# Convolutional mixer on one core: image loads on GpSimd's queue, projection units in eights, and reordered short chains

## The chip, the cores and the metric

The kernel runs on one core of a Trainium2 chip. TensorE (PE in the profile) multiplies matrices into PSUM; VectorE (DVE), ScalarE (ACT) and GpSimd (POOL) work on tiles; SyncE (SP) issues most DMA transfers, ACT and POOL some. The metric is the device time of one execution in microseconds. Three executions of the kernel before gave 3662.24, 3666.53 and 3667.2; the time before is the median, 3666.53 us.

## What is computed

The input is eight images of 384 channels by 32 x 32 positions, in float32. Four layers follow, each `x + f(GroupNorm(x))`:

- layer 0: q, k and v are each a depthwise 3x3 convolution, batch norm over all eight images, exact gelu and a 1x1 convolution; attention over the 1024 positions in 8 heads of 48; an output projection with batch norm over all images;
- layer 1: a gate takes the 2 best of 4 experts for each image; an expert is two 1x1 convolutions with an activation between;
- layer 2: a depthwise 3x3 convolution and a 1x1 convolution, both with weights rounded to -1, 0 and 1;
- layer 3: deformable attention. A depthwise 5x5 convolution of stride 2 on q, gelu and a 1x1 convolution give offsets (through tanh); the image is sampled bilinearly at 16 x 16 shifted points; keys and values come from the samples; 6 heads of 64 attend; a projection follows.

Both batch norms of layer 0 join all images: what follows one cannot start before the last image has gone through what precedes it. An image is 1.57 MB and lies in SBUF as 128 partitions by KC = 3 chunks of 1024.

## The kernel before

**Convolution stage (0 to 366 us).** For each image `norm(b)` gives three functions: `begin` (statistics of the three chunks on DVE by `gn_start`, then `gn_mean`), `middle` (`gn_spread`: matmul `gna`, L115, and two DVE operations) and `end` (`gn_scale`: matmul `gnb`, L126, the power -0.5 on POOL in `rsqrt`, L96, the shift `ss` on DVE, L131; then `affine` on ACT, L145, into one of two padded images `pads`). `stack(b, g)` copies 42 channels, three times shifted by a row, from a pad to a tile `st` of 126 partitions (three DMAs on SP's queue, L319); `left_over` (L340) collects the six channels that nine such groups leave, for four images at a time. A group of `st` is multiplied by a banded weight `cw[:, g]` in 12 matmul instructions of 512 columns (L404), copied by ACT (L410), measured by DVE (L412) and written to `raw` in DRAM, by ACT's DMA queue and for three groups of the last image by POOL's (L427). For every second image, the last three groups are computed on DVE instead (`convolve`, `tap`, L291; `finish`, L298, writes `cst` by SP's queue at L301).

The loop over `work` goes through (image, group) pairs. `stacks(n)` issues copies up to `AHEAD` = 9 groups ahead. `begins` says at which group's turn the next image's `norm` begins; its three functions follow one per turn, and the image after it is then loaded if it is not yet (`load_x`, L241, by `load_image`, L168 to L170). [...] Before this loop stands the order that the change touches:

```
        stacks(2)
        with tc.issue_after(stacked[0].ins):
            load_x(1)
            nc.sync.dma_start(out=cw[:, 3:], in_=i["cw"][:, 3:])
            ident = load_const("ident")
        stacks(AHEAD)
        load_x(2)
```

The first three groups' weights `cw[:, :3]` are loaded at L244, directly behind the first image. `ident` is a 128 x 128 identity used only in a branch not taken.

**Attention (375 to 1785 us).** An image has four pairs of head blocks `pr`, two halves h of the queries and four steps kc of two key blocks each: 32 steps. In a step PE does the scores of the next step (`scores`, L676), ACT the exponential (L683), PE the weighting (`weigh`, L691). Other matmuls of PE lie in a list `todo`: projections of q and k (`project`, L593), values (`values`, L566), the output projection of the image before (`out_project`, L613). At the second step of every half (`kc == NS`, L773), up to four units are taken from it. A unit is three accumulating products, six instructions in the trace, and its result is copied from PSUM by `evac` (ACT or DVE in turn, L77, L79) or DVE. `GELUS` (L561) names the steps of an image, counted from 0, at which ACT applies gelu to a third of the next image (`gelu_chunk`).

**Joint (1785 to 1810 us).** After the last output projection `out_project` with a given `po` copies a bank on ACT, measures it on DVE and sums products with x (`cross`, L509). `norms` (L817 to L850) aggregates with `bn_moments` (L155), makes batch-norm scales and group-norm scales for every image with the matmuls `gmean` and `gvar`.

**Layers 1 to 3 (1810 to 3665 us).** Layers 2 and 3 of image b are a generator; each `yield` gives an estimate of microseconds in which PE is free, and after it as many units of layer 1 of image b + 1 are put in as 2.6 us (`UNIT`) fit. The nine depthwise taps of layer 2 (L1416, L1424) on DVE precede `yield 2.0` (L1426) and the pointwise matmuls `pw` (L1432). In layer 3 the offset products `pom` (L1565) go through tanh on ACT to y, x and mask rows; DVE scales each and adds its grid (L1575, and one `tensor_scalar` after it); ACT forms `1 - |distance|` for x (L1583, L1584) and for eight blocks of y (`wt`, L1597, L1598), POOL multiplies both (L1599), and PE samples with `wt` (`xsb`, L1603). In images 0 to 5 the offset products take one small matmul and go through DRAM. The last two images have no layer 1 beside them and run as a pair. The output's last projection `pf` (L1759) ends in a DVE sum per chunk (L1763) and a DMA per chunk (`put`, L1770).

## Time and profile before

| what | value |
|---|---|
| median of three executions | 3666.53 us |
| profiled execution, its own time | 3666.73 us |
| span of the profile | 3664.9 us |
| mean granted TensorE clock | 0.983 |
| PE busy | 3542.1 us, 97% |
| DVE busy | 1759.0 us, 48% |
| ACT busy | 1268.3 us, 35% |
| POOL busy | 214.0 us, 6% |
| PE busy in 0 to 92, 92 to 184, 184 to 275, 275 to 367 us | 61.42, 83.51, 88.66, 91.40 us |

A line of the timeline gives the start, the time that a run of like instructions took, engine, source line, operation, what it writes and reads, how many, and in brackets the idle time of the engine just before it with what ended it. A matmul product in float32 shows as several instructions. "Waits" add up such idle times by the pair of waiting and releasing work. In a table of windows, busy times of the engines stand first, then the granted TensorE clock as a share, the DMA engines' busy share and the bytes moved per second. The span starts at the first instruction; the execution's own time also holds what lies around it.

### The profile page before, as it was taken

The numbers are of one execution on the slowest core, as the hardware profiler recorded it, in microseconds if no ns is written. First come the engines' busy times: TensorE is split into PE (matmuls) and PEld (weight loads), VectorE is DVE, ScalarE is ACT, GpSimd is POOL, SyncE is SP. The second block draws the span as 40 slices with busy tenths as digits, with TensorE's granted clock in tenths as the row PEclk, the third lists the DMA queues.
The fourth block names the chain that finished last, engine by engine and source line by source line (L and its number), as shares of the span: only waits on it lengthen the run. The fifth ranks groups of instructions, "written<-read, shape, count | busy, mean of one in ns | idle before, by whom it ended". The sixth has DMA issues, their size and how long they took to land.

```text
span 3664.9 us, 38838 instructions
## 1 busy us (share of the span) xinstructions
PE 3542.1 (97%) x15533; PEld 1520.4 (41%) x15533; DVE 1759.0 (48%) x2823; ACT 1268.3 (35%) x1512; POOL 214.0 (6%) x194
## 2 busy tenths in 40 slices
PE   6999999999999999999899999999999999999888
PEld 3444333333333333334444444445344444444434
DVE  6687123242323232323446547474664647557563
ACT  2222454545444454543322321323322232322222
POOL 0101100000000000000000010100102010010112
PEclk9999999999999999999999999999999999999898
DMA  6677211121212021212440010111101001010000
GB/s 227 229 259 274 73 55 52 49 64 38 63 42 78 25 76 27 74 28 74 146 183 23 33 52 21 39 49 34 38 24 56 26 34 49 22 54 19 0 35 18
DMA packets 88746, 252.79 MB, mean 69 GB/s; under 512 B 19754, under 2 KB 20418, under 8 KB 88170
## 3 DMA queue, kind: packets, MB, share of 16 engines
q1 hardware_dynamic: 74832, 210.82, 17.3%
q10 hardware_dynamic: 12120, 37.19, 2.9%
q8 instruction: 127, 2.08, 0.2%
q0 software_dynamic: 1600, 2.15, 0.2%
q14 instruction: 67, 0.55, 0.0%
HBM read 133.44 MB, written 75.59 MB: 57 GB/s over the span
## 4 chain that ended last, share of the span: by engine, by line
PE 40%; DVE 9%; ACT 1%; DMA 0%; issue 0%; POOL 0%; DVEq 0%; POOLq 0%; ACTq 0%; SPq 0%
PE y L1349 12%; PE ph L1328 8%; DVE y L1424 6%; PE pq L1469 3%; PE pf L1759 3%; PE pw L1432 3%; PE pav L1659 2%; PE s L1643 2%; DVE hd L1314 1%; PE pss L1672 1%; PE pk L1617 1%; PE pv L1626 1%; PE xsb L1603 1%; PE px L1492 1%; DVE off L1539 1%; PE plog L1078 0%
## 5 line engine op out<-in xcount | busy, mean ns | idle before, releaser
L683 ACT ACTIVATE p<-s 128x1024 f32<-128x1024 f32 x512 | 497.0, 1021 | 507.8 <-PE s L676 507.0
L1349 PE MATMUL y<-hd,w_sb 128*128 128x512 f32 x1080 | 491.3, 600 | 3.5 <-DVE hd L1314 3.5
L691 PE MATMUL pav<-p,vt 64*64 64x512 f32 x4096 | 488.9, 590 | 0.0
L1328 PE MATMUL ph<-h,w_sb 128*128 128x512 f32 x1104 | 485.0, 594 | 0.2 <-DMA w_sb<-in_w_dram 0.2
L676 PE MATMUL s<-qk,qk 48*64 48x512 f32 x3072 | 371.8, 597 | 3.4 <-ACT p L683 3.4
L404 PE MATMUL pk<-st,cw_sb 126*126 126x512 f32 x720 | 312.7, 595 | 17.7 <-DMA st<-pad 15.4
L1328 PEld LDWEIGHTS ph<-h,w_sb 128*128 128x128 f32 x1104 | 207.5, 190 | 259.1 <-issue 253.9
L1349 PEld LDWEIGHTS y<-hd,w_sb 128*128 128x128 f32 x1080 | 198.8, 191 | 245.5 <-issue 233.9
L691 PEld LDWEIGHTS pav<-p,vt 64*64 64x64 f32 x4096 | 165.1, 133 | 276.6 <-issue 268.4
L652 DVE COPY ta<-pav 128x512 f32<-128x512 f32 (+1 forms) x65 | 44.3, 682 | 411.1 <-PE pav L691 408.1
L1424 DVE SCALAR_TENSOR_TENSOR y<-h,tap,y 128x961 f32<-128x961 f32 (+1 forms) x192 | 234.8, 1249 | 0.6
L1338 ACT ACTIVATE hd<-ph,b_sb 128x512 f32<-128x512 f32 x180 | 122.7, 682 | 315.7 <-PE ph L1328 315.6
L1539 DVE SCALAR_TENSOR_TENSOR off<-q,dw_sb,off 128x225 f32<-128x225 f32 (+3 forms) x432 | 212.5, 553 | 1.6
L404 PEld LDWEIGHTS pk<-st,cw_sb 126*126 126x126 f32 x720 | 136.8, 192 | 183.0 <-issue 176.7
L676 PEld LDWEIGHTS s<-qk,qk 48*64 48x64 f32 x3072 | 112.5, 133 | 227.5 <-issue 184.2
L79 DVE COPY qk<-pq 128x512 f32<-128x512 f32 x48 | 33.2, 692 | 292.2 <-PE pq L593 292.2
L1650 ACT ACTIVATE p<-s 128x1024 f32<-128x1024 f32 x96 | 93.2, 1021 | 191.0 <-PE s L1643 190.9
L410 ACT COPY y<-pk 126x512 f32<-126x512 f32 (+1 forms) x124 | 69.9, 585 | 237.7 <-PE pk L404 119.0
L1314 DVE TENSOR_TENSOR hd<-hd,cb 128x512 f32<-128x512 f32 x180 | 123.3, 690 | 48.2 <-ACT hd L1338 48.0
L1432 PE MATMUL pw<-y,upw 128*128 128x512 f32 x288 | 129.7, 604 | 9.4 <-DVE y L1424 9.4
L1759 PE MATMUL pf<-att,wp_sb 128*128 128x512 f32 x288 | 130.4, 608 | 4.3 <-DVE att L1686 3.8
L1695 POOL TENSOR_TENSOR p<-p,p 128x1024 f32<-128x1024 f32 x48 | 113.0, 2354 | 355.1 <-ACT p L1650 355.1
(295 smaller groups left out, 3838.9 us busy)
## 6 DMA issues: line engine op xcount, KB each, us to landing
g<-raw SPq DMA_DIRECT2D x72, 512.0 KB
st<-pad SPq DMA_DIRECT2D x180, 168.0 KB
raw<-y ACTq DMA_DIRECT2D x171, 168.0 KB
xa<-in_x_dram SPq DMA_DIRECT2D x24, 512.0 KB
xh<-in_x_dram SPq DMA_DIRECT2D x48, 256.0 KB
f<-in_x_dram SPq DMA_DIRECT2D x24, 512.0 KB
f<-o SPq DMA_DIRECT2D x24, 512.0 KB
o<-ot SPq DMA_DIRECT2D x42, 256.0 KB
```

The source lines that it names most:

```text
L404: nc.tensor.matmul(pk[h].rearrange("p (h w) -> p h w", w=W)[: 3 * nch, :, o0 : o0 + c1 - c0], lhsT=lhs, rhs=rhs, start=(k == 0), stop=(k = ...
L676: nc.tensor.matmul(s[64 * k : 64 * k + 64, j * HALF : (j + 1) * HALF], lhsT=kt[r, k0 : k0 + 64], rhs=qt[r, h * HALF : (h + 1) * HALF], sta ...
L683: nc.scalar.activation(p, s, AF.Exp, scale=scale)
L691: nc.tensor.matmul(pav[k][64 * j : 64 * j + 64, :], lhsT=vts[b % 2][r, kc, 2 * hd : 2 * hd + 2, :].rearrange("p a b -> p (a b)"), rhs=p[r, ...
L1314: nc.vector.tensor_tensor(hd, hd, state["cb"], ALU.mult)
L1328: nc.tensor.matmul(ph, lhsT=w1[:, e, c, dc * P : (dc + 1) * P], rhs=state["h1"][c], start=(c == 0), stop=(c == KC - 1),)
L1338: nc.scalar.activation(hd, ph, AF.Relu, bias=b1[:, k : k + 1])
L1349: nc.tensor.matmul(y, lhsT=w2[:, e, dc, m * P : (m + 1) * P], rhs=state[h, k], start=(k == 0), stop=(k == NE * KC - 1),)
L1424: nc.vector.scalar_tensor_tensor(d, f, tap2[:, c, t : t + 1], d, ALU.mult, ALU.add)
L1432: nc.tensor.matmul(pw[h], lhsT=upw2[:, c, m * P : (m + 1) * P], rhs=y[c][:, hs], start=(c == 0), stop=(c == KC - 1),)
L1539: nc.vector.scalar_tensor_tensor(d, f, dw3[:, t : t + 1], d, ALU.mult, ALU.add)
L1759: nc.tensor.matmul(pf[:, hs], lhsT=wp3[:, pr, m * P : (m + 1) * P], rhs=att[:, pr, hs], start=(pr == 0), stop=(pr == NPAIR3 - 1),)
```

## The change

It has six parts.

1. `load_image` takes a queue. Image 1 is loaded by POOL's queue directly behind `cw[:, :3]`; the remaining weights `cw[:, 3:]` and image 2 go on that queue too, held behind the first and the third stack's copies (`behind`). `ident` moves on SP's queue behind the first nine groups.
2. `begins` starts at -3 instead of -1, so that the first norms may begin up to two turns earlier. Image 3 is then loaded at an earlier turn.
3. In attention up to eight units are taken, at the second half (h = 1) only; `GELUS` moves from steps 9, 13, 17 to 5, 13, 21.
4. At the joint, the three aggregates of the output's batch norm come ahead of the last image's `cross` sums; two of these are held behind the first aggregate.
5. `yield 2.0` becomes 3.5. The offsets' rows come in the order x, y, mask; one DVE operation for each of x and y goes, its scale and shift going into ACT's `Abs` (and into the constant `npos`).
6. The last output chunk of the last image is summed and stored in two halves.

```diff
@@ -152,7 +152,7 @@

     def bn_moments(st, j, tiles):

-        nc.vector.bn_aggr(tiles[0][:, j, :], st[:, j, :, :].rearrange("p a b -> p (a b)"))
+        return nc.vector.bn_aggr(tiles[0][:, j, :], st[:, j, :, :].rearrange("p a b -> p (a b)"))

     def bn_params(g, b, tiles):

@@ -165,9 +165,16 @@
         nc.vector.tensor_tensor(sh, b, sh, ALU.subtract)
         return sc, sh

-    def load_image(dst, src):
-        for c in range(KC):
-            nc.sync.dma_start(out=dst[:, c, :], in_=src[:, c, :])
+    def load_image(dst, src, queue=nc.sync):
+        return [queue.dma_start(out=dst[:, c, :], in_=src[:, c, :]) for c in range(KC)]
+
+    def behind(ins, first):
+
+        tc.add_manual_dep(
+            ins.ins, first.ins.name, mybir.DependencyInfo(
+                mybir.DependencyClass.Sync, mybir.DependencyReason.DATA
+            ), reason="transfers in their order",
+        )

     x_img = [i["x"][b].rearrange("(p c) n -> p c n", c=KC) for b in range(B)]
     out_img = [out[b].rearrange("(p c) n -> p c n", c=KC) for b in range(B)]
@@ -234,14 +241,15 @@
         nc.gpsimd.memset(cst, 1.0)
         xts = {}

-        def load_x(b):
+        def load_x(b, queue=nc.sync):
             xts[b] = image(f"xa{b}")
-            load_image(xts[b], x_img[b])
+            return load_image(xts[b], x_img[b], queue)

         load_x(0)
         g4 = load_const("g4")
         cw = wa.tile([3 * GC, NGC, 3, 3 * GC], F32, name="cw_sb")
         nc.sync.dma_start(out=cw[:, :3], in_=i["cw"][:, :3])
+        load_x(1, nc.gpsimd)
         cwv = load_a("cwv")
         cwr = load_a("cwr")
         vst = wa.tile([3 * GC, 3, 2, 6], F32, name="vst")
@@ -351,7 +359,7 @@
         ]
         work = [(b, g) for b in range(B) for g in groups[b]]

-        begins, n = {}, -1
+        begins, n = {}, -3
         for b in range(1, B):
             n = max(n + 3, work.index((b, groups[b][0])) - AHEAD - 2)
             begins[n] = b
@@ -366,13 +374,15 @@
         for f in norm(0):
             f()

-        stacks(2)
-        with tc.issue_after(stacked[0].ins):
-            load_x(1)
-            nc.sync.dma_start(out=cw[:, 3:], in_=i["cw"][:, 3:])
-            ident = load_const("ident")
+        stacks(1)
+        first = stacked[0]
+        stacks(3)
+        rest = nc.gpsimd.dma_start(out=cw[:, 3:], in_=i["cw"][:, 3:])
+        behind(rest, first)
+        for load in load_x(2, nc.gpsimd):
+            behind(load, stacked[0])
         stacks(AHEAD)
-        load_x(2)
+        ident = load_const("ident")
         gb0 = load_a("gb0")
         sel0, sel1, msk, is_v, one3 = (
             load_a(n) for n in ("sel0", "sel1", "msk", "is_v", "one3")
@@ -477,6 +487,7 @@


     ost = const.tile([P, KC, 2 * B, 6], F32, name="ost")
+    sc_o = bn_tiles(P, KC, "out")
     omv = const.tile([P, B, KC, 2], F32, name="omv")
     xo = const.tile([P, B, KC, 2], F32, name="xo")
     gbo, gw, gbias, ewt, sel2 = (load_const(n) for n in ("gbo", "gw", "gbias", "ewt", "sel2"))
@@ -558,7 +569,7 @@

-        GELUS = {s: [(v, c) for c in range(KC)] for v, s in enumerate((9, 13, 17))}
+        GELUS = {s: [(v, c) for c in range(KC)] for v, s in enumerate((5, 13, 21))}

         def values(b, t):
             pv = bank(f"pv{b}_{t}")
@@ -624,6 +635,8 @@
                 nc.scalar.copy(ot, po)
             nc.vector.bn_stats(ost[:, m, 2 * b + h, :], ot if po_new else po)
             (nc.sync if b + 1 < B else nc.scalar).dma_start(out=o_dram[b, :, m, hs], in_=ot)
+            if not po_new:
+                return lambda: cross(b, m, h, xh, ot)
             cross(b, m, h, xh, ot)

         def spare(k, h):
@@ -769,8 +782,8 @@
                     nc.vector.transpose(spare(1, k), spare(0, k))

             early = b == 0 and pr == 0 and h == 0
-            if early or kc == NS:
-                for _ in range(min(2 if early else 4, len(todo))):
+            if early or (h == 1 and kc == NS):
+                for _ in range(min(2 if early else 8, len(todo))):
                     todo.pop(0)()
             if kc == NT8 - NS:
                 turned = normalise(b, pr, h, pav)
@@ -787,8 +800,14 @@
                         pos[m][:, qs], lhsT=wo0[:, c, m * P : (m + 1) * P],
                         rhs=atts[B - 1][:, c, HALF:][:, qs], start=(c == 0), stop=(c == KC - 1),
                     )
+        ends = [out_project(B - 1, m, 1, pos[m]) for m in range(KC)]
         for m in range(KC):
-            out_project(B - 1, m, 1, pos[m])
+            first = bn_moments(ost, m, sc_o)
+        ends[0]()
+
+        with tc.issue_after(first.ins):
+            for end in ends[1:]:
+                end()

         okt = pp.tile([P, B * NU * 16], F32, tag="p", name="okt")
         recf = rec.rearrange("p u q -> p (u q)")
@@ -803,7 +822,6 @@

-    sc_o = bn_tiles(P, KC, "out")
     _, sco, sho = sc_o
     rs1 = const.tile([P, B], F32, name="rs1")
     sf1 = const.tile([P, B], F32, name="sf1")
@@ -814,8 +832,8 @@
     sum_g = const.tile([P, B], F32, name="sum_g")
     mean_g = const.tile([P, B], F32, name="mean_g")

-    def norms():
-        for c in range(KC):
+    def norms(moments):
+        for c in range(KC if moments else 0):
             bn_moments(ost, c, sc_o)
         bn_params(gbo[:, 0, :], gbo[:, 1, :], sc_o)
         sc, sh = (t.unsqueeze(1).to_broadcast([P, B, KC]) for t in (sco, sho))
@@ -850,7 +868,7 @@
                 sb1[:, :, c], rs1, sho[:, c : c + 1], sf1, ALU.mult, ALU.add
             )

-    norms()
+    norms(False)

@@ -982,7 +1000,7 @@
                         hs = slice(h * HALF, (h + 1) * HALF)
                         nc.vector.bn_stats(ost[:, m, 2 * b + h, :], oe[:, m, hs])
                         cross(b, m, h, xe[:, m, hs], oe[:, m, hs])
-            norms()
+            norms(True)
             for (b, t), f in fetched.items():
                 load_image(f, o_dram[b] if t else x_img[b])

@@ -1423,7 +1441,7 @@
                 f = src[:, r0 + dy : r1 + dy, c0 + dx : c1 + dx]
                 nc.vector.scalar_tensor_tensor(d, f, tap2[:, c, t : t + 1], d, ALU.mult, ALU.add)
                 yield 1.25
-        yield 2.0
+        yield 3.5
         for m in range(KC):
             whole, pw = pair(last, f"pw{b}_{m}")
             for h in range(2):
@@ -1560,28 +1578,31 @@
                 nc.sync.dma_start(out=t, in_=om_dram[b, r : r + 1].to_broadcast([P, NG * LS]))
                 om.append(t)
             yield 7.0
-        for r in range(0 if om else 3):
+        for r in () if om else (1, 0, 2):
             po = big(f"pom_{b}_{r}")
             nc.tensor.matmul(po[:, :512], lhsT=pw3[:, r, :], rhs=offf[:, :512], start=True, stop=True)
             nc.tensor.matmul(po[:, 512:768], lhsT=pw3[:, r, :], rhs=offf[:, 512:], start=True, stop=True)
             t = pl.one([P, NG * LS], f"om{r}", f"om{r}_{b}")

             nc.scalar.activation(t, po[:, : NG * LS], AF.Tanh, scale=1.0 if r < 2 else 0.5)
-            om.append(t)
+            om.insert(0 if r == 0 else r, t)
             yield 0.3
-        gy, gx, md = om
-        for r, t in enumerate((gy, gx)):
+        gx, gy, md = om[1], om[0], om[2]
+
+        for r, t in ((1, gx), (0, gy)):
             t3 = t.rearrange("p (g s) -> p g s", g=NG)
             nc.vector.scalar_tensor_tensor(
                 t3, t3, 2.0 / HS, ref3[:, r, :].unsqueeze(1).to_broadcast([P, NG, LS]),
                 ALU.mult, ALU.add,
             )
-            nc.vector.tensor_scalar(t, t, 1.0, 0.5 * (H - 1), ALU.add, ALU.mult)
+
+            if r == 1:
+                nc.scalar.activation(
+                    gx, gx, AF.Abs, bias=npos[:, NT8 : NT8 + 1], scale=0.5 * (H - 1)
+                )
+                nc.scalar.activation(gx, gx, AF.Relu, bias=1.0, scale=-1.0)
         nc.scalar.activation(md, md, AF.Tanh, scale=0.25, bias=quarter)
         nc.vector.tensor_scalar(md, md, 0.5, 0.5, ALU.mult, ALU.add)
-
-        nc.scalar.activation(gx, gx, AF.Abs, bias=npos[:, NT8 : NT8 + 1])
-        nc.scalar.activation(gx, gx, AF.Relu, bias=1.0, scale=-1.0)
         yield 6.0
         xsb = big(f"xsb_{b}")
         xs2 = vbank(f"xs2_{b}")
@@ -1594,7 +1615,9 @@
             i0, i1 = _sample_rows(t)
             sl = slice(i0 * HS, i1 * HS)
             wt = pl.flat([P, NG, (i1 - i0) * HS], f"wt_{b}_{t}")
-            nc.scalar.activation(wt, gy3[:, :, sl], AF.Abs, bias=npos[:, t : t + 1])
+            nc.scalar.activation(
+                wt, gy3[:, :, sl], AF.Abs, bias=npos[:, t : t + 1], scale=0.5 * (H - 1)
+            )
             nc.scalar.activation(wt, wt, AF.Relu, bias=1.0, scale=-1.0)
             nc.gpsimd.tensor_tensor(wt, wt, gx3[:, :, sl], ALU.mult)
             if t == 0:
@@ -1760,14 +1783,18 @@
                         pf[:, hs], lhsT=wp3[:, pr, m * P : (m + 1) * P], rhs=att[:, pr, hs],
                         start=(pr == 0), stop=(pr == NPAIR3 - 1),
                     )
-            nc.vector.scalar_tensor_tensor(
-                xt[:, m, :], pf, pb3[:, m : m + 1], xt[:, m, :], ALU.add, ALU.add
-            )
-            put(m, xt)
+
+            n = 2 if last and m == KC - 1 else 1
+            for k in range(n):
+                ks = slice(k * N // n, (k + 1) * N // n)
+                nc.vector.scalar_tensor_tensor(
+                    xt[:, m, ks], pf[:, ks], pb3[:, m : m + 1], xt[:, m, ks], ALU.add, ALU.add
+                )
+                put(m, xt, ks)
             yield 0.0

     def put_image(b):
-        return lambda m, xt: nc.sync.dma_start(out=out_img[b][:, m, :], in_=xt[:, m, :])
+        return lambda m, xt, ks: nc.sync.dma_start(out=out_img[b][:, m, ks], in_=xt[:, m, ks])

     UNIT = 2.6

@@ -1844,7 +1871,7 @@
                     out=xt, in_=x2_dram[bass.ds(bi, 1)].rearrange("o p c n -> p (o c) n")
                 )

-                def put_any(m, xt):
+                def put_any(m, xt, ks):
                     nc.sync.dma_start(
                         out=out[bass.ds(bi, 1)].rearrange("o (p c) n -> p (o c) n", c=KC)[
                             :, m : m + 1, :
@@ -1965,7 +1992,8 @@
     L["ref3"] = np.broadcast_to(ref, (P, 2, LS))
     part = np.arange(P)
     pos = [-(part // W + t * (P // W)) for t in range(NT8)] + [-(part % W)]
-    L["npos"] = np.stack(pos, axis=1).astype(f)
+
+    L["npos"] = np.stack(pos, axis=1).astype(f) + f(0.5 * (H - 1))
     return {k: np.ascontiguousarray(v) for k, v in L.items()}
```

## The prediction

> **What bounds the kernel now.** The profile's page gives PE 97% of the span of 3664.9 us; the next engine, DVE, has 48%. So the time is PE's matmuls plus what PE waits, and an edit is worth only what it takes from one of the two. I read the table of PE's waits first, then PE's timeline where those waits lie, then the neighbours that set them.
>
> PE's waits (engine, line, releaser: us in total, times, longest):
> ```profile
> PE gna_a L115 <- DVE mv_a L109: 22.8, 2, 13.7
> PE pk L404 <- DMA st<-pad: 15.4, 2, 8.2
> PE pw L1432 <- DVE y L1424: 9.4, 8, 3.0
> ```
> The first two belong to the convolution stage, 0 to 366 us. PE's timeline there (start, us, line, operation, count, idle before):
> ```profile
> 18.18 11.93 PE L404 MATMUL pk<-st,cw_sb 126*126 126x512 f32 x24 [7.24 <-DMA st<-pad]
> 38.26 7.08 PE L404 MATMUL pk<-st,cw_sb 126*126 126x512 f32 x12 [8.16 <-DMA st<-pad]
> ...
> 60.90 5.29 PE L404 MATMUL pk<-st,cw_sb 126*126 126x512 f32 x12
> ...
> 100.23 0.56 PE L115 MATMUL gna_a<-mv_a,g_sb 128*128 128x2 f32 x2 [13.65 <-DVE mv_a L109]
> 100.66 8.31 PE L404 MATMUL pk<-st,cw_sb 126*126 126x512 f32 x12
> ```
> Two holes, 8.16 us and 13.65 us, and after each the next 12 matmuls are slow: 7.08 and 8.31 us. Steady, a group of 12 starts every 5.15 us (66.17 us on, 48 matmuls in 20.42 us). The windows say why (PE, PEld, DVE, ACT, POOL busy, granted clock, DMA share, GB/s):
> ```profile
> 38.30:45.00 6.70, 6.70 (x12) 3.01 (x13) 2.83 (x4) 0.58 (x1) 0.00 (x0) 0.73 0.68 230
> 100.00:110.00 10.00, 9.77 (x19) 4.65 (x20) 8.35 (x14) 1.17 (x2) 0.55 (x1) 0.66 0.34 113
> ```
> The granted clock is 0.73 and 0.66 there. So a hole costs its length and then 1.93 us (7.08 − 5.15) or 3.16 us (8.31 − 5.15): 8.16 + 1.93 + 13.65 + 3.16 = 26.9 us.
>
> **The first hole: loads off SP's queue.** In the SP timeline the third group's copies (`st`, L319) are issued at 33.44, behind image 1's load (20.33), the rest of `cw` (22.17) and `ident` (33.05), which waited 10.4 us for an ACT-queue write. Afterwards image 1, the rest of `cw` and image 2 go out on POOL's queue, `ident` follows the first nine groups, and SP goes from the first stacks to the next. A group is 3 copies of 168 KB, 0.50 MB; at the stage's some 300 GB/s (below) that is 1.7 us, against 5.15 us of PE. Shared in thirds with ACT's writes and POOL's loads it is 5.0 us: just enough while POOL's 2.7 MB (`cw` rest 1.14, image 2 1.57) last, 27 us. The three groups that land ahead of image 2 are the cover; I charge 1 us (0 to 4), and remove 8.16 + 1.93.
>
> **The second hole: the fourth image.** Image 3's load leaves SP at 89.42, behind 18 copies from 64.10 and the `cst` copies of 84.66; its statistics end on DVE just before 100.23. Afterwards its three DMAs stand between the stacks of groups 6 and 7 of image 1, which I place at 60 to 71 us, so it lands by about 77 us (issue to end took 8.6 us before: 89.42 to 98). PE asks at 86.6 − 8.16 − 1.93 + 4.4 = 81 us. The margin of 4 us holds 5 us of DVE statistics (94.71 to 99.7) only partly: 0 to 5 us may stay. I take 1.5 off: 13.65 + 3.16 − 1.5.
>
> **What the new order delays.** DVE's order in the changed program puts the six statistics of image 1 and their aggregate ahead of the last step of image 0's norm, which before stood here:
> ```profile
> 11.80 0.16 DVE L131 SCALAR_TENSOR_TENSOR ss_a<-ga_a,ss_a 128x1 f32<-128x1 f32 x1 [0.67 <-POOL ss_a L96]
> ```
> Behind it wait ACT's affines (11.99), the first copies (13.26) and PE (18.18): the whole stage. So the kernel cannot start before image 1 has landed. POOL can issue it after its memsets, at 7.16, by 8.7 (0.50 us an issue). 1.57 MB at the 312 GB/s that the window from 2 to 9.5 us shows is 5.0 us, with some 1.2 us of earlier loads ahead: the last chunk lands at about 14.6, two statistics and the aggregate take 1.7, so L131 runs at 16.3 and the start is 4.4 us late. Here a rule speaks against the change. The Trainium skill, "DMA: Bandwidth & Descriptors", section "Issuing engine by pattern", gives simple loads to SP, and GpSimd's path costs about 2.0 us plus bytes/436e3 ("Anatomy of one DMA — SWDGE (gpsimd) path"). An estimate from that page is 3.2 us for the last 512 KB chunk after the others' 2.4 us: landing near 13.5, a delay of 3. This trace's only POOL loads are smaller and slower (KB each, then median us to landing):
> ```profile
> raw<-y POOLq DMA_DIRECT2D x9, 168.0 KB, 7.1
> ```
> 7.1 us for 168 KB, with other traffic, would put the last chunk at 15.8 or, if the bytes add, at 18: a delay of 5.5 to 8. The row is the nearer to a chip with its queues full, but these writes go to DRAM; I keep 4.4 from the byte rate and the range 2 to 8. The first matmuls are equally cold before and after.
>
> Stage sum: 8.16 + 1.93 − 1 + 13.65 + 3.16 − 1.5 − 4.4 = **20.0 us gained** (10 to 25).
>
> **Units in eights (L773).** Between attention steps PE takes blocks of projection units. PE's timeline (matmul groups, all of image 1's kind):
> ```profile
> 625.62 1.90 PE L691 MATMUL pav<-p,vt 64*64 64x512 f32 x16
> 627.45 5.42 PE L613 MATMUL po<-att,wo_sb 128*128 128x512 f32 x12
> 632.71 5.31 PE L593 MATMUL pq<-g,wk_sb 128*128 128x512 f32 x12
> ...
> 645.06 1.90 PE L676 MATMUL s<-qk,qk 48*64 48x512 f32 x16
> 646.78 1.90 PE L691 MATMUL pav<-p,vt 64*64 64x512 f32 x16
> ...
> 650.22 1.90 PE L691 MATMUL pav<-p,vt 64*64 64x512 f32 x16
> 652.05 5.42 PE L593 MATMUL pq<-g,wq_sb 128*128 128x512 f32 x12
> ...
> 664.51 1.90 PE L676 MATMUL s<-qk,qk 48*64 48x512 f32 x16
> ```
> A regular interval is 1.72 us (646.78 − 645.06). From 625.62 to 645.06 are five intervals and 24 matmuls: 19.44 − 8.60 = 10.84. From 650.22 to 664.51, five intervals and 12: 14.29 − 8.60 = 5.69. Twice 5.69 less 10.84 leaves **0.54 us that a block costs whatever its size**. Counting the program's order, 58 blocks become 37: 21 × 0.54 = **11.3 us gained**. The skill's "TensorEngine Tiling (Array Packing)", section "Key Properties", has a reason: changing the tiling mode drains TensorE. Its price is not there; from "TensorE: Matmul & The Clock Gate", section "Single matmul latency", a matmul that cannot overlap costs 166 ns more, and two changes a block make 0.33: 21 × 0.33 = 7.0. The row is measured in place and holds the whole break in the stream, so 11.3. Range 6 to 13.
>
> The cover: the gelu of the next image moves to steps 5, 13 and 21, ahead of such blocks. ACT then does a table load and three gelus, 1.28 + 3.50 us (627.03 to 631.8), before it copies a first unit out of PSUM. PE reaches the bank needing that copy about 5.2 us after the block begins: it fits by 0.4 us. Were it not to fit, 7 images × 2 blocks × up to 1 us; I charge 0. At step 5 the values' gelu also needs its image loaded, 17 us of steps and a block after the load starts: enough for 1.57 MB.
>
> **Statistics before the joint (L624).** The three aggregates of the output's batch norm move ahead of the `cross` sums; the same DVE work stands in another order in one unbroken run (1783.51 to 1790.94), and the chain to `gmean` (7.0 us of PE wait) still needs all of it. 0, ±0.5.
>
> **`yield 2.0` to 3.5 (L1426).** A further result unit of layer 1 (6 matmuls, 2.58 us) comes before the pointwise matmuls, which now wait 1.03 us in six images. That gains some 0.7 each, 4.2. But units run out one earlier: attention's last pair in those images loses its filler, as in the last image, where it waits 0.27 and 0.48 us: −0.75 × 6 = −4.5. Net 0, ±4.
>
> **Offsets (L1575 and on).** Two DVE operations (0.56 + 0.55 us) go, their scale folded into ACT's Abs; the x row comes first. In the last image they stand in the chain to `xsb` (4.40 us wait at 3586.93), of which y's one is hidden by x's ACT steps now started earlier: −0.5. In the image before, DVE's taps bound it: −0.2. Elsewhere layer 1 covers them. Total **0.7** (0 to 2).
>
> **Last chunk in halves (L1763).** The last sum takes 1.28 us (3656.99) and its store is issued at 3658.3, 6.6 us before the span's end. In halves the last sum is 0.69 us (the 128x512 DVE rows) and the last store 256 KB instead of 512 KB: 0.6 + 0.4 = **1.0** (0.3 to 2).
>
> **Sum.** 20.0 + 11.3 + 0 + 0 + 0.7 + 1.0 = 33.0. Span 3664.9 − 33 = 3632; the profiled execution took 3666.73, 1.8 more. The median shown is 3666.53, 0.2 below that execution, so **3634** (3633.5 rounded). Likeliest case's own range: 3626 to 3641.
>
> **Rivals.** (1) The first norm waits 8 us and the fourth image comes 6 us late with a cold clock behind it: the stage gives 26.9 − 8 − 6 − 3 = 10 instead of 20, time 3644. For it: the POOL row above, and SP's semaphore waits on ACT-queue writes (10.4 us at 22.6), which can hit image 3's load again. Against: the DMA share in the two windows, 0.68 and 0.34, leaves room.
> (2) Merging does nothing: PE's break is ACT's evacuation and the exponentials' restart rather than the change of mode, and a longer block meets them as before: 3634 + 11.3 = 3645. For it: ACT's table load of 1.28 us after each gelu block stands in the restart (639.15). Against: the 0.54 also comes out of blocks with copies on DVE (24 matmuls, 128x384: 16.88 us from 669.66).
> (3) It ends slower: POOL's image 1 lands late. Every us of its lateness is a us of PE, since L131 stands behind it in DVE's order. Slower by 7.3 needs 33 + 7.3 = 40 us beyond the assumed 14.6, a landing at 55; at 60 us the time is 3679. For it: POOL's power operation takes 0.55 us at 51.00 but 1.39 at 66.67 while DVE is busy, so POOL is held up at times. Against: the longest POOL landing in the trace is 8.2 us.
> (4) The change doesn't do what it says: both (1) and (2), with image 2's early load taking the bandwidth of the first stacks: 3657 to 3666.
>
> **How the numbers follow.** Likeliest 0.55, (1) 0.20, (2) 0.13, (3) 0.03, (4) 0.09. The range goes from all gains at their bounds (25 + 13 + 4 + 2 + 2 = 46, cut to 44 as they do not all come: 3622) to past (1) and (2): 3650. This kernel's measurement tells 0.2%, 7.3 us. Faster takes in all but (3) and about half of (4): 0.92; same 0.05, slower 0.03.
>
> **What would show it.** Right: PE's row for `st` in the waits under 2 us after the start; the wait for `mv_a` under 6; first L404 at 21 to 26; 37 blocks, block cost 0.5 each; last store of 256 KB. Wrong: a first L404 beyond 28, a new hole at image 3's `gna_a`, PE waiting for a PSUM bank in the first unit of a block, or restarts after eights longer than after fours.

## The result and the profile after

The changed kernel takes 3644.70 us (median of five executions, 3643.82 to 3650.53) against 3666.53 before (five executions, 3662.24 to 3668.54): a ratio of 0.9947, 95% interval 0.9935 to 0.9958. That is 21.8 us faster, where 32.5 were forecast (3634); it lies inside the range of 3622 to 3650, but outside the 3626 to 3641 of the case held likeliest. The profiled span (one execution of each kernel) fell from 3664.9 to 3641.9 us, by 23.0. Marks on PE's timelines cut these 23.0 us into stages:

| stage, from mark to mark | before | after | change | forecast |
|---|---|---|---|---|
| start to first attention scores | 389.75 | 385.10 | -4.65 | -20.0 |
| to the matmul `gmean` (attention and joint) | 1402.80 | 1388.46 | -14.34 | -11.3 |
| to the last image's `pf` (layers 1 to 3) | 1848.68 | 1845.30 | -3.38 | -0.7 |
| to the end of the span (last output) | 23.67 | 23.04 | -0.63 | -1.0 |

(Marks: scores at 389.75 and 385.10; `gmean` at 1792.55 and 1773.56; `pf` at 3641.23 and 3618.86.) The convolution stage gave 15 us less than forecast, the others 5 us more. The runs below show how well one execution's stages can be read. Attention repeats within 1.2 us over the kernels with its old code (1401.61 to 1402.80) and within 0.3 over all but one of those with its new code (1388.26 to 1388.55; the one left out, `eights_old_gelu`, has other gelu steps). The convolution stage repeats less well: its old code gave 389.75 here, and 393.31 and 392.60 in `eights_only` and `eights_old_gelu`.

PE's waits of the changed kernel (engine, line, releaser: us in total, times, longest; line numbers moved, the convolution's matmul is L414):
```profile
PE gna_a L115 <- DVE mv_a L109: 16.8, 3, 9.1
PE pk L414 <- DMA st<-pad: 11.6, 1, 11.6
```
The longest wait for `mv_a`, 9.1, and the 11.6 for `st` both lie before the first group (the start of the stage); the second hole of before has split into three. PE's timeline shows where:
```profile
22.46 7.31 PE L414 MATMUL pk<-st,cw_sb 126*126 126x512 f32 x12 [11.59 <-DMA st<-pad]
...
85.39 0.56 PE L115 MATMUL gna_a<-mv_a,g_sb 128*128 128x2 f32 x2 [3.58 <-DVE xmv L142]
85.81 8.06 PE L414 MATMUL pk<-st,cw_sb 126*126 126x512 f32 x12
...
175.99 0.56 PE L115 MATMUL gna_a<-mv_a,g_sb 128*128 128x2 f32 x2 [5.42 <-DVE mv_a L109]
176.40 7.15 PE L414 MATMUL pk<-st,cw_sb 126*126 126x512 f32 x12
...
257.55 0.35 PE L115 MATMUL gna_a<-mv_a,g_sb 128*128 128x2 f32 x2 [2.31 <-DVE mv_a L109]
257.79 6.98 PE L414 MATMUL pk<-st,cw_sb 126*126 126x512 f32 x12
```
The first hole is gone and the first group starts at 22.46, 4.28 us late (forecast 4.4). But a hole of 3.58 us stays before image 3, and new ones of 5.42 and 2.31 us stand before images 5 and 7, each followed by a slow group. Up to image 4's `gna` (154.41 before, 139.32 after) 15.1 us are won; after it most of them are given back, down to 4.65.

Why a hole before image 5? Its load's issue on SP's queue, before and then after (start, us, engine, line, operation):
```profile
167.31 1.49 SPq L170 DMA_DIRECT2D xa<-in_x_dram  x3
```
```profile
162.09 2.00 SPq L169 DMA_DIRECT2D xa<-in_x_dram  x3
```
At image 4's `gna` PE had come 15.1 us earlier; image 5's load came only 5.2 us earlier. How little room it had had in the kernel before is seen where its statistics end on DVE and where PE asks for them:
```profile
182.24 0.32 DVE L109 BATCH_NORM_AGGREGATE mv_a<-st_a 128x2 f32<-128x36 f32 x1
```
```profile
185.49 0.28 PE L115 MATMUL gna_a<-mv_a,g_sb 128*128 128x2 f32 x2
```
The statistics were complete some 3 us before PE used them.

### The profile page after: what moved, and what is told of

The parts are those of the page before. It is cut to its first block, busy times and chain, and to the rows that moved or that the text cites. A ratio compares the mean times of both kernels' runs of the same rounds, so it can differ in the third digit from the quotient of the medians.

```text
span 3641.9 us, 38824 instructions
## 1 busy us (share of the span) xinstructions
PE 3533.7 (97%) x15533; PEld 1537.9 (42%) x15533; DVE 1752.0 (48%) x2808; ACT 1267.4 (35%) x1512; POOL 218.1 (6%) x201
## 4 chain that ended last, share of the span: by engine, by line
PE 47%; DVE 2%; ACT 1%; POOL 1%; issue 0%; DMA 0%; DVEq 0%; POOLq 0%; ACTq 0%
PE ph L1346 14%; PE y L1367 14%; PE pq L1487 3%; PE pw L1450 3%; PE pf L1782 3%; PE s L1666 2%; PE pav L1682 2%; PE pk L1640 1%; PE pss L1695 1%; PE pv L1649 1%; PE xsb L1626 1%; PE plog L1096 1%; DVE off L1557 1%; DVE y L1442 1%; POOL p L1718 1%; ACT p L1673 1%
## 5 line engine op out<-in xcount | busy, mean ns | idle before, releaser
L414 PE MATMUL pk<-st,cw_sb 126*126 126x512 f32 x720 | 314.7, 598 | 12.3 <-DMA st<-pad 11.6
L414 PEld LDWEIGHTS pk<-st,cw_sb 126*126 126x126 f32 x720 | 137.9, 193 | 178.4 <-issue 175.1
L604 PE MATMUL pq<-g,wq_sb 128*128 128x512 f32 x288 | 129.7, 601 | 2.5 <-DMA wq_sb<-in_wq_dram 2.5
```

Of the source, the lines that this page charges most:

```text
L414: nc.tensor.matmul(pk[h].rearrange("p (h w) -> p h w", w=W)[: 3 * nch, :, o0 : o0 + c1 - c0], lhsT=lhs, rhs=rhs, start=(k == 0), stop=(k = ...
L604: nc.tensor.matmul(pq, lhsT=w_in[v][:, c, pr * P : (pr + 1) * P], rhs=acts[b][v][:, c, h * HALF : (h + 1) * HALF], start=(c == 0), stop=(c ...
```

## The experiments

All edits are to the changed kernel unless it says "the kernel before". The median of the kernel before, measured beside the runs, was 3665.67 for `conv_only`, `eights_only`, `start` and `loads_pool`, 3666.16 for `early_sp`, `early_pool`, `raw_pool` and `eights_old_gelu`, and 3666.85 for the other four. For the convolution stage the mark is the time of the first attention scores.

**Parts 1 and 2 alone, on the kernel before (`conv_only`).** The edit is the diff up to `ident = load_const("ident")`.

> The kernel before with parts 1 and 2 alone (loads on POOL's queue, norms begun earlier). Theory (SP's queue, held up by landings of the writes to raw, sets the pace of the convolution stage, so holes filled early come back at images 5 and 7): 4 us faster than before, time about 3662, PE's first attention scores about 4 us earlier than 389.75, holes of some 5 and 2 us before gna of images 5 and 7. Rival (the stage gained its 20 us and another part of the change, acting earlier than thought, took them back): about 3646.

Measured: 3663.31, ratio 0.9989 (0.998 to 0.9998). The holes stand where they were foretold: 5.06 us before image 3, 6.78 before image 5, 2.44 before image 7. In the profiled execution, the slowest of twelve (3667.07), the first scores came at 390.20, no earlier than before (389.75), with the first group at 23.08. So the two parts alone are worth some 1 to 7 us by the interval, and nothing later in the kernel took 20 us back: attention and layers take 1402.39 and 1849.11 us, as before. The rival falls.

**Part 3 alone, on the kernel before (`eights_only`).**
```diff
-GELUS = {s: [(v, c) for c in range(KC)] for v, s in enumerate((9, 13, 17))}
+GELUS = {s: [(v, c) for c in range(KC)] for v, s in enumerate((5, 13, 21))}
...
-            if early or kc == NS:
-                for _ in range(min(2 if early else 4, len(todo))):
+            if early or (h == 1 and kc == NS):
+                for _ in range(min(2 if early else 8, len(todo))):
```

> The kernel before with part 3 alone (eights, gelu at steps 5, 13, 21). Theory (21 blocks fewer at 0.34 us, the cost of a block that no gelu precedes, and the end of the one stall that the old gelu step 17 makes in image 0, 3.25 us with its slow matmuls and the 1.1 us wait for ql): 14.5 us faster, 3652. Rival (every block costs the forecast 0.54 us, nothing else): 11.3 us faster, 3655, with image 0's stall at the old place.

Measured: 3651.96, ratio 0.9963 (0.9948 to 0.9977), 13.7 us faster: the theory's 14.5, though the interval (8 to 19 us) holds the rival's 11.3 too. What separates them is in the trace. From the first scores to `gmean` it takes 1388.26 us instead of 1402.80, 14.5 us less (and since part 4 is not in this run, that part's share of the changed kernel's 14.3 is nothing, as forecast). Scores no longer wait for ACT anywhere, and these two lines of the kernel before, the stall in image 0, have no counterpart:
```profile
483.34 3.69 PE L676 MATMUL s<-qk,qk 48*64 48x512 f32 x16 [3.25 <-ACT p L683]
486.80 3.00 PE L691 MATMUL pav<-p,vt 64*64 64x512 f32 x16
```
At step 17 of image 0 there are no units left, so ACT's gelu with its two table loads (476.15 to 482.26) had no PE work to hide behind: 3.25 us of idle time, then matmuls 1.79 and 1.10 us slower than the usual 1.90.

**Eights with the gelu left at steps 9, 13 and 17, on the kernel before (`eights_old_gelu`).** The edit is that of part 3 without its first two lines.

> The kernel before with units in eights but the gelu left at steps 9, 13, 17. Theory (a gelu with its two table loads needs a block of PE work behind it, as image 0's stall of 3.25 us with slow matmuls at step 17 shows): steps 9 and 17 of seven images stall PE by 5 to 6 us each, 13 more than before: 65 to 75 us slower than before less 7 for the blocks, about 3725. Rival (ACT has slack to absorb it): about 3655.

Measured: 3730.68 (one execution), 64.5 us slower than before, within the 58 to 68 expected (65 to 75 less 7 for the blocks). PE's waits name the cause:
```profile
PE s L676 <- ACT p L683: 45.6, 14, 3.3
```
Fourteen stalls of 3.3 us, two in each of seven images, where the kernel before has 3.4 us in all. From the first scores to `gmean` it takes 1463.81 us, 61.0 more than before; the rest of the loss lies in the convolution stage, whose code is the same. With 7.2 for the blocks saved, 68.2 us have to be explained. The stalls give 42.2 of them, and 26.0 are left, 2.0 us per new stall; in this trace the slow matmuls behind the fourteen stalls lose 1.7 to 3.1 us each, 2.2 on average. ACT has no slack for a gelu without a block. The eights pay only with the gelu steps moved.

**The start delay taken out (`start`).** Image 1's statistics are ordered behind the last step of image 0's norm (L131), kept in `shift[0]` (a list made ahead of it).
```diff
-        nc.vector.scalar_tensor_tensor(
+        shift[0] = nc.vector.scalar_tensor_tensor(
...
-                for c in range(KC):
-                    st = gn_start(xt, f"a{b}", c, st)
+                with tc.issue_after(shift[0].ins) if b == 1 else nullcontext():
+                    for c in range(KC):
+                        st = gn_start(xt, f"a{b}", c, st)
```

> The changed kernel with DVE's statistics of image 1 put behind the last step of image 0's norm (L131), so that the first matmuls of the convolution start at about 18.2 instead of 22.46. Theory (the stage is paced by SP's queue, and the norms of images 3, 5 and 7 wait for loads whose place is behind it): nearly all of the 4.3 us is lost again in the holes before images 3, 5 and 7; 0 to 1.5 us faster than the changed kernel, 3643 to 3645. Rival (the start delay is paid in full at the end): 4.3 us faster, 3640.

Measured: 3641.98, ratio 0.9935 (0.9919 to 0.9952), which cannot be told from the changed kernel's 0.9947 and lies between the two expectations. The trace of one execution (3643.70) is plainer: the first group starts at 18.59 instead of 22.46, and the first scores come at 385.39 instead of 385.10. All of the 3.9 us is lost again in the holes (3.65, 8.03 and 2.30 us before images 3, 5, 7), as the theory said. Image 7's load left SP no earlier (245.13 for 245.11). Image 5's did, by 3.0 us (159.12 for 162.09), yet its statistics were complete only 0.6 us earlier (174.93 for 175.54): DVE waited for the second chunk, and did 2.97 us of convolution work ahead of the third chunk's statistics (170.17 to 173.14). So DVE's order has a share in that hole; no run changes it alone.

**The later loads on POOL's queue (`loads_pool`).**
```diff
-                    load_x(b2 + 1)
+                    load_x(b2 + 1, nc.gpsimd)
```

> The changed kernel with the loads of images 3 to 7 on POOL's queue as well. Theory A (the holes before images 3, 5 and 7 are the loads' place in SP's queue): holes of 3.6, 5.4 and 2.3 us and their slow matmuls (2.9, 2.0, 1.8 us) go, 15 to 18 us faster than the changed kernel, about 3628. Theory B (the DMA engines' bytes are the bound): the same idle time appears as PE's wait for st, at most 4 us faster, 3641 or more.

Measured: 3645.40, ratio 0.9946 (0.9929 to 0.9962): no gain. Neither theory was right as put. The holes before images 5 and 7 are gone: from 154.19 to the first scores at 385.56 it takes 231.4 us, against 245.2 in the changed kernel from the same place (139.86). But 14.3 us had been lost before that place. POOL issued all five images as soon as buffers were free, and a window (PE, PEld, DVE, ACT, POOL busy, granted clock, DMA share, GB/s) shows the burst:
```profile
52.00:66.00 14.00, 5.40 (x13) 2.30 (x13) 7.94 (x23) 1.66 (x3) 1.28 (x3) 0.81 1.00 375
```
The DMA engines are full and DVE, whose order puts statistics of images 3 and 4 ahead of image 2's last norm steps, waits for those loads, with PE behind it (8.52 us of idle time before 65.88). So earlier loads remove the holes of images 5 and 7, and there is bandwidth (375 GB/s against 252 on average in the changed kernel's first 92 us); but loads that come in a burst cost as much as they save.

**Each load one norm earlier, on SP's queue (`early_sp`).**
```diff
-                if b2 + 1 < B and b2 + 1 not in xts:
-                    load_x(b2 + 1)
+                if b2 + 2 < B and b2 + 2 not in xts:
+                    loads = load_x(b2 + 2)
```

> The changed kernel with each of the loads of images 3 to 7 one norm earlier in SP's order (image b + 2 where norm b begins); no other queue, no more bytes. Theory (the holes before images 3, 5 and 7 are the loads' place in SP's queue, and the DMA engines have room: up to 375 GB/s in the run with POOL's loads against 252 on average): the holes with their slow matmuls, 17 to 18 us in all, go; PE's first attention scores at 368 to 373 instead of 385.1, time about 3630. Rival (bytes or SP's issue rate bound the stage): PE waits for st instead, 3640 or more.

Measured: 3634.88, ratio 0.9912 (0.9894 to 0.9929), some 10 us faster than the changed kernel. First scores at 376.39, 8.7 us earlier. Image 5's load now leaves SP at 118.31. The place of image 5's norm on PE's timeline, which had a hole of 5.42 us:
```profile
129.98 12.02 PE L414 MATMUL pk<-st,cw_sb 126*126 126x512 f32 x24 [2.54 <-DMA st<-pad]
...
172.50 0.28 PE L115 MATMUL gna_a<-mv_a,g_sb 128*128 128x2 f32 x2
172.64 5.29 PE L414 MATMUL pk<-st,cw_sb 126*126 126x512 f32 x12
```
No hole and no slow group stands at this `gna`, nor at those of images 3 and 7. The 18.1 us of holes and slow groups (3.58 + 2.91, 5.42 + 2.00, 2.31 + 1.83) are gone, but only half of them is gained. PE now waits four times for `st`, 1.2 to 2.5 us each, 6.8 in all (the total of 18.2 less the 11.44 of the start); 1.7 us go in the slow group behind the longest of these waits (12.02 us for 24 matmuls, elsewhere 10.33), and 0.9 us more at image 7's `gnb` (1.56 for 0.65). That a load moved forward in SP's queue pushes the copies behind it back could explain three of the four waits and is not shown; the first (1.76 us before 47.81) stands in `conv_only` and `start` too (1.61 and 1.01), where no such load was moved. The theory's 3630 was too good; the truth lies between it and the rival.

**The same on POOL's queue, each load held behind the latest stack copy (`early_pool`).**
```diff
-                if b2 + 1 < B and b2 + 1 not in xts:
-                    load_x(b2 + 1)
+                if b2 + 2 < B and b2 + 2 not in xts:
+                    loads = load_x(b2 + 2, nc.gpsimd)
+                    for load in loads:
+                        behind(load, stacked[0])
```

> The same loads one norm earlier, on POOL's queue, each held behind the latest issued stack copy. Theory: as with SP, about 3630, if the holding keeps the loads apart; if POOL's powers of the norms wait behind held loads, new holes at gnb and st of up to 5 us each and 3640.

Measured: 3640.75 (one execution), the second reading's time, but not by its mechanism. PE idles 3.64 us before 63.08 and 1.60 before 99.88, each time for DVE's `ve`, a step of a norm; POOL's power follows `ve` within 0.4 us both times (63.21, 100.00), so it does not wait behind loads. It is `ve` that is late: on DVE it stands behind statistics of a later image, which waited 3.42 and 1.54 us for its load, and the second time behind convolution work too. This is what the burst above did. First scores at 380.52, 4 us later than with the loads on SP.

**The same on SP, on the kernel before (`before_early`).** The edit is that of `early_sp`, on the lines of the kernel before.

> The kernel before with the loads of images 3 to 7 one norm earlier on SP, and nothing else. Theory (the place of the load in SP's order makes the hole before image 3): that hole of 13.65 us with its 3.16 us of slow matmuls goes, the first hole of 8.16 us stays, and no new holes come before images 5 and 7; 15 to 17 us faster than before, about 3650. Rival (POOL's queue is needed for it): 3658 or more.

Measured: 3659.88, ratio 0.9979 (0.9972 to 0.9987): 7 us faster, where 15 to 17 were expected. The hole before image 3 is gone (`gna` at 92.11 without a wait, 100.23 before) and none comes before images 5 and 7, as expected; but other waits take most of the 16.8 us back. PE's largest wait in the stage:
```profile
PE pk L404 <- DMA st<-pad: 22.2, 6, 8.4
```
That is 6.8 us more than before (15.4, two waits). With 2.71 us for a copy of ACT, a start 0.7 us later and 1.8 us more before the first projection, the 16.8 shrink to some 5, and the first scores come 5.25 us earlier (384.50). SP's load of image 3 now stands directly behind image 2's, 8.44 us of issue from 45.72, and image 1's first copies come behind both. So parts 1 and 2 are worth having after all, not by themselves but beside the early loads: with them the first scores come at 376.39, without them at 384.50. That this is due to the room which POOL's queue makes in SP's is likely and not shown, since no run has the queue without the earlier norms.

**The start delay and the early loads together (`start_early`).** Both edits above.

> The changed kernel with both edits: image 1's statistics behind L131 on DVE, and the loads of images 3 to 7 one norm earlier on SP. Theory (with the holes gone, the start delay of 4.3 us is no longer hidden by anything and is worth its whole length): 4 us faster than with the early loads alone, about 3631. Rival (the stage has again a bound behind the holes, SP's or the DMA engines'): 3634 to 3636, with PE's waits for st grown by some 4 us.

Measured: 3629.60, ratio 0.990 (0.9884 to 0.9917). It beats both kernels: 37 us faster than before, and 5.3 us faster than with the early loads alone (by the medians; the intervals of the two ratios overlap, the executions do not: 3626.73 to 3632.21 against 3632.41 to 3635.45). First scores at 370.4, 6 us earlier than there. The same 3.9 us of start that were worth nothing with the holes in place are now worth their whole length; the 2 us beyond are within what this stage varies by. PE's waits for `st` behind the start fell to one of 1.59 us, though 4.6 us of waits for ACT's copies and for writes appear.

**Writes to `raw` on POOL's queue, without and with those of the DVE convolutions (`raw_pool`, `raw_all_pool`).**
```diff
-                queue = nc.gpsimd if b == B - 1 and g in (5, 6, 7) else nc.scalar
+                queue = nc.gpsimd
```
and in the second run also
```diff
-                nc.scalar.dma_start(out=raw[v][b, : 3 * GC, KC - 1, :], in_=y)
+                nc.gpsimd.dma_start(out=raw[v][b, : 3 * GC, KC - 1, :], in_=y)
```

> The changed kernel with all writes to raw on POOL's queue[...]. Theory (SP is held by landings of raw, 53.8 us of its waits): SP runs ahead of PE, the loads of images 3, 5 and 7 are issued 10 us or more earlier against PE, the holes shrink by half or more, 6 to 15 us faster, 3630 to 3639. Rival (SP's place against PE is set by something else, such as the release of st): the holes stay, 3643 to 3648.

> The changed kernel with all writes to raw, those of the DVE convolutions too, on POOL's queue, so that SP waits for none of them. Theory (SP was held by writes[...]): SP's 84 us of waits for raw<-yv of the run before go, its loads of images 3, 5 and 7 come early, the holes shrink by half or more, 3630 to 3639. Rival (SP is held by other things, or POOL's norms are now held by the writes): holes of 5 us or more stay, 3644 or more.

Measured: 3675.45 and 3670.20 (one execution each), far slower than the changed kernel; the second lies within the executions of the kernel before (3663.99 to 3671.06). SP's waits for `raw<-y` in the stage, 70.2 us in the kernel before and 79.6 in the changed one, are gone from both, yet holes of 10.8, 11.6 and 10.5 us stand before images 3, 5 and 7. In the first run SP waits 84.2 us for `raw<-yv` instead. In the second it waits for none of them, but 51.4 us for ACT's padded images, and the load of image 3 leaves at 74.38, no earlier than 73.79; moreover DVE takes up image 3's statistics only at 87.83, behind convolution taps that it had been given first. These edits changed the order on DVE and POOL as well, so they do not show what holds SP. The theory that the writes do is not supported, and the question stays open.

**`yield 2.0` as before (`yield_old`).**
```diff
-        yield 3.5
+        yield 2.0
```

> The changed kernel with yield 2.0 in layer 2, as before. Forecast theory: nothing changes in the sum (pw waits again 1.03 us in six images, pav and pss lose their waits), span 3641 to 3643. Other reading, from the changed kernel's waits (pw 9.4 to 3.2, pav and pss 3.9 to 8.4): 1.7 us slower, span about 3643.6.

Measured: span 3641.9, that of the changed kernel, and `gmean` to `pf` takes the same 1845.3 us. The first reading is right: the six waits for `pw` come back (9.4 us for 3.2), those for `pav` and `pss` go (3.9 for 8.4), and the sum is nothing.

## Why the prediction was right and where it failed

**Direction and range: right, the range with luck.** Every part acted with the sign forecast or none. But the largest term, the convolution stage, fell outside its own range (4.65 us for 10 to 25), and the total stayed inside because the other stages gave 5 us more. Rival (1) had named 3644, nearly the time measured, and had the fourth image late with a slow group behind it; its sum did not come true either (a stage of 10 us, a first norm 8 us late for 4.3, image 3 late by 6 us for 3.58). Of the prediction's own signs of being right, the wait for `mv_a` under 6 us (7.7 behind the start) and the 0.5 us of a block were not met; of its signs of being wrong, a hole at image 3's `gna` stood, as a rest of the old one.

**The start delay: right.** 4.28 us for 4.4. L131 ran at 16.19 (forecast 16.3): POOL issued image 1 at 7.11, and the last chunk was in use at 14.62. The rate of bytes was the proper measure; the row of 7.1 us for 168 KB was not. The estimate from the Trainium skill's page, "DMA: Bandwidth & Descriptors", section "Anatomy of one DMA — SWDGE (gpsimd) path", gave 3 us, less near. The first matmuls lost about as much as before (2.0 us in the first 12; 1.6 in the first 24 before).

**The first hole: right.** It went as a whole with its slow group. PE waited once more for 0.48 us (45.83), for a write. (`ident` left SP at 4.17, ahead of the copies and not behind the first nine groups as the change's description has it.)

**"I take 1.5 off" for the fourth image: wrong.** The load was to leave SP at 60 to 71 us and left here:
```profile
73.79 2.19 SPq L169 DMA_DIRECT2D xa<-in_x_dram  x3
```
PE asked at 81.8 (forecast 81) and had to wait 3.58 us, then lost 8.06 - 5.15 = 2.91 in the slow group: 6.5 us instead of 1.5. I had let SP's copies follow PE's progress further than they did.

**"Stage sum 20.0": wrong, and this is the main failure.** The sum ended with the second hole, as if what PE gains by image 4 were kept. It was not: 5.42 + 2.00 before image 5, 2.31 + 1.83 before image 7 and 0.65 at its `gnb`, 12.2 us that were not in the sum, less 2.0 of the 2.28 us of idle time before 234.01 in the kernel before. From 15.1 us won at image 4, that leaves 4.9; the trace has 4.65 at the first scores. In the kernel before the loads of images 5 and 7 had been early enough only because PE had been held up twice. I priced the holes and never asked by how much the next loads were early. The number was there: image 5's load left SP at 167.31, and its `gna` came at 185.49 with statistics ended at 182.2, 3 us of slack against 15 us that I wished to take; image 7's had 4 us (260.6 to 264.6). `start` shows an earlier start lost in the holes (3.9 us earlier in, none out), `early_sp` and `start_early` that the holes go when the loads stand earlier in the queue. How much of the hole before image 5 is the load and how much DVE's order behind it is not separated, and what gives SP its pace is not shown.

**Attention: near in sum, wrong in its parts.** The 21 blocks fewer are right. **"0.54 us that a block costs whatever its size" is too much.** An image that had seven blocks and now has four took 174.89 us (578.64 to 753.53) and takes 173.86 (581.43 to 755.29): 1.03 / 3 = 0.34 us a block. Both blocks that I had compared stood at gelu steps, whose restart is slower for another reason:
```profile
639.72 1.90 PE L691 MATMUL pav<-p,vt 64*64 64x512 f32 x16
641.52 2.00 PE L676 MATMUL s<-qk,qk 48*64 48x512 f32 x16
643.34 1.90 PE L691 MATMUL pav<-p,vt 64*64 64x512 f32 x16
```
The intervals around the second of these lines are 1.80 and 1.82 instead of 1.72, 0.18 us that follow ACT's table load and do not occur behind the blocks without a gelu; gelu steps are three per image before and after, so that part is not saved. 21 x 0.34 = 7.2 us. The price estimated from the Trainium skill, "TensorE: Matmul & The Clock Gate", section "Single matmul latency" (0.33 a block, 7.0 us), which I weighed and set aside for the row, came nearer. That can be chance: the page's figure is for bf16 and these matmuls are float32, and no run separates the drain from other costs of a block. The other 7 us, which the sum did not have, come from image 0: 3.25 + 1.79 + 1.10 at step 17 and 1.14 at the wait for `ql`, and I had looked for what the new gelu steps might cost, not for what the old ones did. The cover of 0.4 us that I found for the first evacuation of a block held: no scores and no units wait.

**Layers: 3.4 for 0.7.** The `yield` was forecast at 0 and is 0, in part by luck. The forecast had its gain and its loss in the same six images; in the traces the new `yield` gains 2.3 us up to the first `pom` of the last two images (1642.30 us behind `gmean`, 1644.62 with the old one), and the last two images give it back. So the 3.4 us are there with the old `yield` too. In that run the stretch from the first `pom` to the first `xsb`, which the shortened chain of the offsets fills, takes 11.71 us instead of 13.27 in the last image but one and 10.58 instead of 11.59 in the last: 2.6 us for the 0.7 forecast. The term was too small above all in the last image but one, put at 0.2; there `xsb` waits 0.6 us less (7.33 for 7.94), and a wait of 0.69 us of the norm's `gnb_d` is gone. The last image's `xsb` waits 3.88 us in the changed kernel instead of 4.40, as forecast. The remaining 0.8 us I did not isolate.

**Last output: 0.63 for 1.0.** The two halves' sums take 1.41 us together and not 1.28, since the first half is not started sooner. The stretch repeats within 0.2 us (23.5 to 23.7 in five kernels without the halves, 23.0 to 23.1 in five with them); in the four runs that put still more transfers on POOL's queue it took 24.2 us or more, for which I have no cause.

## What to carry to other kernels

A wait that PE is relieved of must be followed past the place where it stood: list the next loads, and for each the slack between its landing and its use. The smallest slack, with what that load itself moves forward, is about what an earlier gain can keep (here 3.3 + 5.2 us for image 5, at whose `gna` 9.5 us were kept). A fixed cost is to be measured on two cases that differ in nothing else, and a rate of issue that another engine sets must not be assumed to speed up with the engine that waits for it.

## What the hardware showed unexpectedly

What a hole costs in slow matmuls does not follow from its length. Behind 13.65 us of idle time (before) the next 12 matmuls lost 3.16 us, behind 3.58 us 2.91, behind 2.31 us 1.83; yet behind 2.28 us (before, ahead of 234.01) and 2.71 us (`before_early`, ahead of 81.92) they lost nothing. The traces show a pattern behind it. The granted clock changes only at points that lie a multiple of 3.41 us apart, and the record has it full or at half. The hole of 2.31 us (255.24 to 257.55) fell into one step of that grid (255.25 to 258.66), and the clock was halved in the next. The hole of 2.28 us (231.73 to 234.01) was cut by an edge at 233.04, and the clock stayed full. The windows of the changed kernel, then of the kernel before (PE's busy time is the first after the length, the granted clock third from the end):
```profile
255.30:258.60 3.30, 1.05 (x4) 0.72 (x5) 2.80 (x6) 0.33 (x1) 0.00 (x0) 1.00 0.83 273
258.70:262.00 3.30, 3.30 (x5) 1.35 (x4) 3.30 (x4) 0.15 (x1) 0.00 (x0) 0.50 0.74 250
```
```profile
229.70:233.00 3.30, 2.03 (x7) 0.95 (x5) 3.27 (x5) 0.00 (x0) 0.00 (x0) 1.00 0.29 83
233.10:236.40 3.30, 2.39 (x6) 1.23 (x7) 2.83 (x8) 1.02 (x2) 0.00 (x0) 1.00 0.90 317
```
Counted over the fourteen traces, each without its first and last 30 us and without gaps under 0.3 us, a full-clock step in which PE idled 2.0 us or more was followed by half the clock in all 134 cases, one with 0.7 to 1.5 us in none of 89, and one between in 14 of 53. What a hole then costs is about half of the halved time left behind it: 6.0, 4.2 and 3.4 us were left behind the changed kernel's three holes, and 2.91, 2.00 and 1.83 lost. So the same idle time is cheap or dear by where it falls.

The DMA engines moved 375 GB/s while POOL's loads and SP's copies ran together, well above the 312 that I had taken as the best; the kernel before itself moved 364 from 340 to 370 us, where I had not looked.
